# A macaron layer on one core: C spread by the matrix engine from three bf16 parts, expert results weighed where they leave PSUM, and gathered by an adding DMA

## The chip, the cores and the metric

The program runs on one core of one Trainium2 chip. The metric is the device time of one execution in microseconds (us). Its engines are TensorE (PE, with its weight loads as PEld), VectorE (DVE), ScalarE (ACT), GpSimd (POOL) and SyncE (SP), which only issues DMAs here. PE clock figures are shares of full speed as the profile shows them granted.

## What is computed

The input x holds 2 sequences of 2048 rows of 128 numbers. Three sublayers follow one another, each on the layer norm of x and added to it:

```
x = x + 0.5 * ffn(layernorm(x))     # 32 experts, 4 of them per row, and 4 shared chunks
x = x + ssm(layernorm(x))           # 256 channels, 16 states
x = x + 0.5 * ffn(layernorm(x))     # the same weights again

ffn: scores = softmax(x router^T); the best 4, divided by their sum
     out = sum over the 4 of weight * down(silu(gate x) * up x), plus the shared expert
ssm: u, z = silu(...); B, C = u W_x + b_x; dt = softplus(u W_dt + b_dt)
     h_t = h_{t-1} * exp(dt_t * A) + dt_t * u_t * B_t        # 16 states per channel
     y_t = sum over the 16 states of h_t * C_t, plus D * u_t; out = (y * z) W_out + b_out
```

All of it is in fp32.

## The kernel before

**Tiles.** x stays in SBUF as 8 blocks `xb[b]` of 512 rows (4 tiles of 128 rows). Blocks 0 to 3 are the first sequence, 4 to 7 the second.

**The expert sublayers** (`mixture`, L498) take the blocks in groups, `GROUPS` (L36): 0-1, 2-3 and 4-7 in the first, 0-3, 4-5 and 6-7 in the second. A group is routed on DVE (L548 to L720): every row's 4 experts, and for each a place in a list sorted by expert and padded so that 128 places have one expert. POOL scatters the normed rows `xn` to those places in `xs` in DRAM, one indirect DMA for each tile and choice (L761, 256 in all). The experts go in batches of 4 times 128 places (112 in all, 56 per sublayer): SP loads `xs` (L856), PE turns it (`pt_x`, L866), ACT copies it out of PSUM (L869), PE does gate and up in two halves (`gu`, L883), with the offsets of the weights loaded to registers from `sl` (L875), ACT does the silu (L895), DVE multiplies (L901), PE turns again (`pt_h`), ACT copies (L910), PE does down (`oq`, L915), ACT copies the result (L924), SP stores it to `ys`. Then POOL gathers the 4 results of each row (L944, 256 DMAs into `yg`), and DVE multiplies each with its weight `wk` and adds it to x (L958, 256 instructions). `wk` comes from L730 to L738. The shared expert (L797 to L836) adds to x on its own.

**The state space** (`state_space`, L1007) goes block by block. A prologue makes u, z, B and C (`ps_b`, L1049, 32 rows: 16 of B, 16 of C) and dt. B and C are stored to DRAM (L1068). For each of the 16 states, 128 steps over the 8 blocks: SP spreads the row of B over 128 partitions by a DMA from DRAM (`bs`, L1144) and the row of C too (`cs`, L1179); POOL multiplies dt*u by B (L1155, "drive"); ACT makes the two decays in PSUM (`da`, L1167); DVE runs two scans over 512 columns (L1194) and multiplies the states by C (L1207, 128x1024, `hst` and `cs` both in SBUF); PE adds the product, turned, to `y` in PSUM (L997). An epilogue gates, projects and adds to x.

**What sets the order.** Every piece is an `op` with an engine, a guessed cost, reads, writes and a priority. `Plan.run` (L147) plays them through once at build time and fixes each engine's order; the priorities in `FIRST`, `SECOND` and `BLOCKS` (L47 to L67) decide between pieces that could start at the same time. Each engine then runs its list strictly in order. `RINGS` (L38) gives the number of buffers of each kind; PSUM has 8 banks: `y` takes 2, `da` 2, `gu` 2, `w` (everything else) 2.

Of the kernel before, what the change touches and what calls it, by code (L numbers as in the profile page):

```python
# [29 lines left out]
S = 16  # L30
SQ = 4
# [7 lines left out]
    y=1, da=2, gu=2, w=2,  # L39
    xn=4, xnT=3, rt=1, lo=1, sc=1, mr=1, mk=1, cum=1, sm=1, route=3,  # L40
    shb=1, sg=2, hs=4, xs=3, xT=2, h=2, hT=2, yq=2, yg=2,
    pro=1, u=1, z=1, xnTs=1, t2=4, dt=2, dtu=2, bs=3, cs=3, hst=3,
# [5 lines left out]
    (-688.4, -610.7, (-1306.1, 24.95), 852.9, (-570.4, 166.01), (1470.8, 462.55)),  # L48
    (295.5, 12697.4, (-3985.4, 43.35), 4958.0, (-3337.9, 135.87), (-392.6, 253.65)),
    (15.1, -395.6, (12799.2, 79.27), -483.9, (-450.5, 7.10), (-438.3, 144.71)),  # L50
)
SECOND = (
    (-1574.4, -939.9, (652.6, 0.03), -1436.8, (-3869.3, 0.78), (2227.8, 203.49)),
    (-546.7, 12169.7, (3525.1, 83.68), -3253.9, (480.7, 378.95), (14344.2, 162.64)),
    (-1606.9, 12399.2, (902.0, 249.98), -512.2, (916.6, 0.00), (852.9, 148.58)),
# [3 lines left out]
    (-4279.5, 84.48),  # L59
    (-631.7, 0.50),  # L60
    (-608.5, 34.66),
    (64.0, 1.83),
    (-3035.2, 283.21),
    (-3171.2, 11.49),
    (-4049.9, 104.09),
    (-323.4, 156.10),
# [23 lines left out]
class Plan:  # L90
# [4 lines left out]
    NEAR, LAG, SWITCH, DMA, TURN, AGE = 0.0625, 0.2, 1.3, 2.3, 0.8000, 0.0900  # L95
# [106 lines left out]
def macaron_kernel(  # L202
# [41 lines left out]
        for k in ("y", "da", "gu", "w")  # L244
# [61 lines left out]
    xb = [load(f"x{b}", xf[b], [P, TB, D], (-1000, b)) for b in range(NBLK)]  # L306
# [28 lines left out]
    zero = buf("t2", [P, SQ * D], name="zero")  # L335
    op("dve", 0.5, lambda: nc.vector.memset(zero.t, 0.0), w=[zero], prio=(-1, 0))
    rows, buf_of = {}, {}
    for li, layer in enumerate(GROUPS):
        seen = {}
        for gi, blocks in enumerate(layer):  # L340
            n = len(blocks)
            k = seen.get(n, 0)
            seen[n] = k + 1
            buf_of[li, gi] = (n, k)
            if (n, k) not in rows:
                rows[n, k] = [dram_buf(f"{v}{n}{k}", [slots(blocks) * P, D]) for v in ("xs", "ys")]

    def clear_rows(key, prio):
        b = rows[key][0]
        v = b.t.rearrange("(c p r) d -> c p (r d)", p=P, r=SQ)  # L350
        for c in range(v.shape[0]):
            op(
                "sp",
                0.8,
                lambda c=c: nc.sync.dma_start(v[c], zero.t),
                r=[zero],
                p=[b],
                prio=prio,
                size=4 * P * SQ * D,
            )  # L360
# [10 lines left out]
    for i, key in enumerate(order_of_rows[1:]):  # L371
        clear_rows(key, (-900, 10 * i + 4))
# [4 lines left out]
    wx = load("wx", w_x, [P, ND, 2 * S], late)  # L377
    bx = load("bx", b_x, [2 * S, 1], late)
# [24 lines left out]
    nc.gpsimd.iota(iota_p.t, [[0, 1]], channel_multiplier=1, allow_small_or_imprecise_dtypes=True)  # L403

# [55 lines left out]
    def ln_apply(v, b, dst, prio, hold=()):  # L460
        mv, rs, nb, mvs, rss = stat[v]

        def f():
            for t in range(TB):
                i = b * TB + t
                nc.scalar.activation(
                    dst.t[:, t, :],
# [6 lines left out]
        op("act", 1.15, f, r=[xb[b], rss[b]], w=[dst], hold=hold, prio=prio)  # L474

    def transposed(src, ring, dst_ring, prio, name):
# [3 lines left out]
        def f():  # L480
            for t in range(TB):
                nc.tensor.transpose(pt.t[:, t, :], src.t[:, t, :], ident.t)
# [15 lines left out]
    def mixture(li, gi, pr):  # L498
# [7 lines left out]
        if li == 0:  # L506
            for b in blocks:
                op("dve", 1.75, lambda b=b: ln_stats(v, b), r=[xb[b]], w=[stat[v][3][b]], prio=p)
# [4 lines left out]
        for i, b in enumerate(blocks):  # L513
            xns[b] = buf("xn", [P, TB, D])
# [163 lines left out]
        idx_b, sl_b, wk_b = Buf(), Buf(), Buf()  # L678
# [4 lines left out]
        def indices():  # L683
# [5 lines left out]
            route["wk"] = sbuf[3].tile([P, NTM, TOPK], F32, tag="wk", name="wk")[:, :NT, :]  # L689
# [7 lines left out]
        def owners():  # L697
# [4 lines left out]
            nc.vector.tensor_scalar(ej, ej, float(E - 1), 3.0 * H, ALU.min, ALU.mult)  # L702

            den = sm_tile("den", [P, NTM])[:, :NT]
            nc.vector.tensor_reduce(den, sm["m8"][:, :NT, :TOPK], AX.X, ALU.add)
            nc.vector.reciprocal(den, den)
            nc.vector.tensor_scalar(den, den, 0.5, None, ALU.mult)

        op("dve", 1.3, owners, w=[smb], prio=p)
# [9 lines left out]
        def slot_list():  # L719
            nc.vector.tensor_copy(route["sl"], ejT.t[0:1, :NSL])  # L720

        op("dve", 0.25, slot_list, r=[ejT, route_b], w=[sl_b], prio=p)
        pw = pr["weigh"]

        for k in range(TOPK):
            eq = buf("lo", [P, NTM, E], name="eq", part=lambda t: t[:, :NT, :])

            def weigh(k=k, eq=eq):
                p8 = sm["p8"][:, :NT, :]
                nc.vector.tensor_tensor(  # L730
                    eq.t, posm.t, p8[:, :, k : k + 1].to_broadcast([P, NT, E]), ALU.is_equal
                )
                nc.vector.tensor_tensor(eq.t, eq.t, sc.t[:, :, :E], ALU.mult)
                nc.vector.tensor_reduce(route["wk"][:, :, k], eq.t, AX.X, ALU.add)
                if k == TOPK - 1:
                    wk = route["wk"]
                    den = sm["den"][:, :NT]
                    nc.vector.tensor_tensor(  # L738
                        wk, wk, den.unsqueeze(2).to_broadcast([P, NT, TOPK]), ALU.mult
                    )  # L740

            op(
                "dve",
                2.05 * f,
                weigh,
                r=[posm, sc, smb, route_b],
                w=[eq],
                p=[wk_b],
                hold=[turn_b],
                prio=pw,  # L750
            )
# [35 lines left out]
        for b in blocks:  # L787
# [3 lines left out]
            for c in range(NSH):  # L791
                w = w_all[:, E + c, :]
                gp, up = buf("gu", [P, T], name="gp"), buf("gu", [P, T], name="up")
# [27 lines left out]
            def down(o=o, hs=hs):  # L821
# [18 lines left out]
                w=[xb[b]],  # L840
# [6 lines left out]
        for q in range(NSL // SQ):  # L847
            pe_ = (*pr["experts"](q), q)
            xs = buf("xs", [P, SQ, D])
# [10 lines left out]
                size=4 * P * SQ * D,  # L860
# [3 lines left out]
            def turn(dst_, src_):  # L864
                for s in range(SQ):
                    nc.tensor.transpose(dst_.t[:, s, :], src_.t[:, s, :], ident.t)  # L866
# [3 lines left out]
            for s0 in range(0, SQ, 2):  # L870
                gu, sg = buf("gu", [P, 2, 2 * H], name="gu"), buf("sg", [P, 2, H], name="sgq")
# [52 lines left out]
            op("act", 0.59, lambda a=yq, b=o: nc.scalar.copy(a.t, b.t), r=[o], w=[yq], prio=pe_)  # L924
# [11 lines left out]
        for i, b in enumerate(blocks):  # L936
            for t in range(TB):
                pc = pr["combine"](i * TB + t)
                yg = buf("yg", [P, TOPK, D])
                for k in range(TOPK):  # L940

                    def gather(i=i, t=t, k=k, yg=yg):
                        pool(
                            nc.gpsimd.indirect_dma_start(  # L944
                                out=yg.t[:, k, :],
# [4 lines left out]
                                ),  # L950
                            )
                        )

                    op("pool", 1.26, gather, r=[ys_b, idx_b, route_b], p=[yg], prio=pc, lag=2.5)

                def add(i=i, b=b, t=t, yg=yg):
                    for k in range(TOPK):
                        nc.vector.scalar_tensor_tensor(  # L958
                            xb[b].t[:, t, :],
                            yg.t[:, k, :],  # L960
                            route["wk"][:, i * TB + t, k : k + 1],
                            xb[b].t[:, t, :],
                            ALU.mult,
                            ALU.add,
                        )
                    if li == 0:
                        ln_stats("b", b, t, t + 1)

                op(
                    "dve",  # L970
                    1.4 + (0.44 if li == 0 else 0.0),
                    add,
                    r=[yg, wk_b, route_b],
                    w=[xb[b]],
                    p=[stat["b"][3][b]] if li == 0 else [],
                    prio=pc,
                )
            if li == 1:
# [4 lines left out]
                    r=[xb[b]],  # L983
# [23 lines left out]
    def state_space(b, rank):  # L1007
# [36 lines left out]

        ps = buf("w", [2 * S, T], name="ps_b")

# [6 lines left out]
        bc = buf("t2", [2 * S, T], name="bc")  # L1053
# [12 lines left out]
        def store_b():  # L1066
            bd_t["t"] = rows2.tile([2 * S, T], F32, tag="bd", name="bd")
            nc.sync.dma_start(bd_t["t"], bc.t)  # L1068

        op("sp", 0.8, store_b, r=[bc], w=[bd], prio=pp, size=8 * S * T)  # L1070
# [66 lines left out]
        for s in range(S):  # L1137
# [24 lines left out]
            for k in range(ND):  # L1162
                da = buf("da", [P, T], place=ND * n + k)

                def decay(s=s, k=k, da=da):
# [9 lines left out]
            cb = buf("cs", [P, T], place=n)  # L1175
            op(
                "sp",
                0.8,
                lambda s=s, cb=cb: nc.sync.dma_start(  # L1179
                    cb.t,  # L1180
                    bd_t["t"][S + s : S + s + 1, :]
                    .rearrange("o t -> (o t)")
                    .partition_broadcast(P),
                ),
                r=[bd],
                w=[cb],
                prio=rank(s - 3),
                size=4 * P * T,
            )
            for k in range(ND):  # L1190
# [12 lines left out]
                op("dve", 1.3, scan, r=[das[k], st_b[s]], w=[h], prio=ps_)  # L1203
# [10 lines left out]
            op("dve", 1.6, times_c, r=[cb], w=[h], prio=ps_)  # L1214
# [24 lines left out]
        for i in range(2):  # L1239
# [57 lines left out]
            op("dve", 1.3, added, r=[po], w=[xb[b]], p=[stat["c"][3][b]], prio=pe_)  # L1297
# [69 lines left out]
```

## Time and profile before

| | before |
|---|---|
| median of 5 runs | 1641.74 us (1632.44 to 1642.64) |
| the profiled execution | 1642.64 us, span 1640.9 us, PE clock 0.80 |
| busy, us: PE / DVE / POOL / ACT | 1063.9 / 1031.5 / 905.7 / 812.4 |

The span is the time from the first to the last instruction; the 1.7 us around it belong to the launch. By the first and the last step of each block the span falls into four stages, and the profile gives the busy time of each engine in each of them:

| stage, us | what runs | PE | DVE | ACT | POOL |
|---|---|---|---|---|---|
| 0 to 393 | loads, routing, first group's experts | 245.5 | 134.4 | 125.7 | 158.0 |
| 393 to 814 | state space of blocks 0 to 3, experts of the first sublayer | 289.1 | 374.7 | 295.7 | 270.2 |
| 814 to 1348 | blocks 4 to 7, experts of the second sublayer | 358.4 | 435.1 | 306.0 | 345.8 |
| 1348 to 1641 | the last groups' experts | 170.9 | 87.4 | 85.0 | 131.8 |

### The profile page before, as it was taken

The page shows a single profiled execution, that of the slowest core. Times are in us where ns is not written, and L with a number is a line of the kernel's source. Part 1 is how long each engine was busy: PE and PEld are TensorE (multiplying, and loading weights), DVE is VectorE, ACT ScalarE, POOL GpSimd, SP SyncE. Part 2 cuts the span into 40 slices and gives each one's busy share as a digit, 9 for nine tenths or more (in the row PEclk, how much of TensorE's full clock was granted, in tenths as well). Part 3 has the DMA queues.
Part 4 walks back from the last instruction along what each step waited for, and adds up shares of the span by engine and source line. Part 5 has one row for each costly group of instructions (what it writes and reads, how often), then busy time and mean ns, then how long its engine had stood idle before and what let it go on. Part 6 is the DMA issues. An engine that isn't in the chain of part 4 may idle for free.

```text
span 1640.9 us, 18009 instructions
## 1 busy us (share of the span) xinstructions
PE 1063.9 (65%) x5202; PEld 792.4 (48%) x5202; DVE 1031.5 (63%) x1741; ACT 812.4 (50%) x1428; POOL 905.7 (55%) x702
## 2 busy tenths in 40 slices
PE   6496184777666778682767753575778786186781
PEld 3264072555555556571444432454567565165561
DVE  5346032243989989988798779748989955022232
ACT  3242061247877759781572652256778844043320
POOL 1605607266557755738664778655894463714435
PEclk9698597898989879795777975587979987687896
DMA  9812132244455436543331133224555532234422
GB/s 306 314 52 71 53 98 67 75 106 138 142 143 150 139 90 168 146 125 97 89 98 54 57 102 106 86 66 133 152 155 161 155 92 72 71 100 111 120 65 51
DMA packets 204257, 187.81 MB, mean 114 GB/s; under 512 B 18690, under 2 KB 155523, under 8 KB 204163
## 3 DMA queue, kind: packets, MB, share of 16 engines
q1 hardware_dynamic: 187778, 153.09, 31.8%
q0 software_dynamic: 16384, 33.59, 7.2%
q8 instruction: 45, 0.74, 0.2%
q14 instruction: 50, 0.40, 0.1%
HBM read 123.16 MB, written 63.44 MB: 114 GB/s over the span
## 4 chain that ended last, share of the span: by engine, by line
PE 31%; DVE 27%; issue 17%; another core or an unknown queue 11%; ACT 8%; POOL 2%; DMA 2%; SPq 1%; DVEq 0%; POOLq 0%; ACTq 0%
DVE hst L1194 11%; PE gu L883 8%; DVE hst L1207 4%; PE oq L915 4%; PE o L824 3%; DVE x L958 3%; PE gp L797 2%; PE up L797 2%; ACT L294 2%; PE pt_h L866 2%; PE pt_x L866 2%; PE ps_o L1281 2%; PE y L997 2%; DVE h L901 1%
## 5 line engine op out<-in xcount | busy, mean ns | idle before, releaser
L1155 POOL TENSOR_TENSOR hst<-dtu,bs 128x1024 f32<-128x1024 f32 x128 | 307.4, 2411 | 218.2 <-PE y L997 171.6
L761 POOL DMA_INDIRECT xs<-xn,idx x256 | 272.0, 1062 | 238.9 <-DVE le L699 78.1
L944 POOL DMA_INDIRECT yg<-ys,idx x256 | 254.3, 993 | 243.4 <-DVE x L958 147.8
L883 PE MATMUL gu<-w_all,xT 128*128 x896 | 271.0, 438 | 44.3 <-DVE h L901 27.6
L997 PE MATMUL y<-ident,hst 128*128 128x128 f32 x1024 | 168.0, 319 | 179.2 <-DVE hst L1207 161.4
L1207 DVE TENSOR_TENSOR hst<-hst,cs 128x1024 f32<-128x1024 f32 x128 | 276.1, 2157 | 3.6
L901 DVE TENSOR_TENSOR h<-sgq,gu 128x256 f32<-128x256 f32 x224 | 89.1, 414 | 294.9 <-ACT sgq L895 193.5
L1194 DVE TENSOR_TENSOR_SCAN hst<-da,st,hst 128x512 f32<-128x512 f32 x192 | 237.6, 1267 | 13.5 <-ACT da L1167 12.9
L997 PEld LDWEIGHTS y<-ident,hst 128*128 128x128 f32 x1024 | 140.1, 166 | 217.7 <-issue 217.3
L1167 ACT ACTIVATE da<-dt,a 128x512 f32<-128x512 f32 x256 | 172.8, 688 | 110.5 <-DVE hst L1194 106.0
L883 PEld LDWEIGHTS gu<-w_all,xT 128*128 128x128 f32 x896 | 182.9, 222 | 84.2 <-DVE h L901 32.8
L915 PE MATMUL oq<-w_all,hT 128*128 x896 | 142.0, 309 | 103.2 <-ACT hT L910 55.4
L915 PEld LDWEIGHTS oq<-w_all,hT 128*128 128x128 f32 x896 | 128.4, 217 | 131.3 <-ACT hT L910 72.6
L294 ACT ACT_TABLE_LOAD x144 | 184.8, 1283 | 3.3 <-PEq L1355 0.8
L895 ACT ACTIVATE sgq<-gu 128x256 f32<-128x256 f32 x224 | 82.3, 384 | 136.5 <-PE gu L883 61.5
L958 DVE SCALAR_TENSOR_TENSOR x<-yg,wk,x 128x128 f32<-128x128 f32 x256 | 121.9, 477 | 33.0 <-DMA yg<-ys,idx 26.8
L924 ACT COPY yq<-oq 128x512 f32<-128x512 f32 x112 | 65.2, 583 | 121.3 <-remote 68.3
L866 PE MATMUL pt_h<-ident,h 128*128 128x128 f32 x448 | 84.7, 311 | 51.8 <-DVE h L901 23.7
L806 ACT ACTIVATE sg<-gp 128x512 f32<-128x512 f32 x64 | 38.2, 597 | 152.1 <-PE gp L797 87.3
L910 ACT COPY hT<-pt_h 128x512 f32<-128x512 f32 x112 | 65.1, 584 | 83.9 <-PE pt_h L866 43.9
L866 PEld LDWEIGHTS pt_h<-ident,h 128*128 128x128 f32 x448 | 61.2, 160 | 78.2 <-issue 35.0
L812 DVE TENSOR_TENSOR hs<-sg,up 128x512 f32<-128x512 f32 x64 | 44.1, 690 | 84.1 <-PE up L797 37.8
(133 smaller groups left out, 1438.7 us busy)
## 6 DMA issues: line engine op xcount, KB each, us to landing
bs<-bd SPq DMA_DIRECT2D x128, 256.0 KB
cs<-bd SPq DMA_DIRECT2D x128, 256.0 KB
xs<-xs SPq DMA_DIRECT2D x112, 256.0 KB
ys<-yq SPq DMA_DIRECT2D x112, 256.0 KB
xs<-zero SPq DMA_DIRECT2D x56, 256.0 KB
xs<-xn,idx POOLq DMA_INDIRECT x256
yg<-ys,idx POOLq DMA_INDIRECT x256
x<-in_x SPq DMA_DIRECT2D x8, 256.0 KB
```

The lines of the kernel that those rows point to most:

```text
L294: nc.scalar.preload_act_table_set(name)
L761: nc.gpsimd.indirect_dma_start(out=xs_b.t, out_offset=bass.IndirectOffsetOnAxis(ap=route["idx"][:, i * TB + t, k : k + 1], axis=0), in_=xn ...
L866: nc.tensor.transpose(dst_.t[:, s, :], src_.t[:, s, :], ident.t)
L883: nc.tensor.matmul(gu.t[:, s, :], xT.t[:, s0 + s, :], w_flat[:, bass.ds(offs["v"][s0 + s], 2 * H)], start=True, stop=True,)
L915: nc.tensor.matmul(o.t[:, s, :], hT.t[:, s, :], w_flat[:, bass.ds(offs["v"][s] + 2 * H, D)], start=True, stop=True,)
L944: nc.gpsimd.indirect_dma_start(out=yg.t[:, k, :], out_offset=None, in_=ys_b.t, in_offset=bass.IndirectOffsetOnAxis(ap=route["idx"][:, i * ...
L958: nc.vector.scalar_tensor_tensor(xb[b].t[:, t, :], yg.t[:, k, :], route["wk"][:, i * TB + t, k : k + 1], xb[b].t[:, t, :], ALU.mult, ALU.add,)
L997: nc.tensor.matmul(y[:, t, k * P : (k + 1) * P], src[:, k, t * P : (t + 1) * P], ident.t, is_transpose=True, start=start and k == 0 and t ...
L1155: nc.gpsimd.tensor_tensor(h.t[:, :, 1:], dtu.t, bs.t.unsqueeze(1).to_broadcast([P, ND, T]), ALU.mult)
L1167: nc.scalar.activation(da.t, dt.t[:, k, :], AF.Exp, scale=a_t.t[:, k, s : s + 1])
L1194: nc.vector.tensor_tensor_scan(h.t[:, k, 1:], da.t, h.t[:, k, 1:], 0.0 if ini else st_sb[:, k, s : s + 1], ALU.mult, ALU.add,)
L1207: nc.vector.tensor_tensor(h.t[:, :, :T], h.t[:, :, 1:], cb.t.unsqueeze(1).to_broadcast([P, ND, T]), ALU.mult,)
```

## The change

1. **C by PE.** `W_x` and its bias are laid out so that the product has 128 rows: C, B, C and C, each at the start of a quarter. The three copies of C become three bf16 parts that add up to C (two more ACT copies and two DVE subtractions per block). For each step one bf16 matmul with a matrix of zeros and ones adds the three parts and spreads them over 128 partitions of PSUM (`c`, one bank). L1179 goes; the multiplication reads C from PSUM.
2. **Weights travel with the rows.** Rows of `xn` and `xs` have 160 numbers, 128 and the 32 weights of the experts (zero where not chosen). L730 to L738 go; a shorter calculation writes the weights before the scatter. After the down matmul, ACT loads four column numbers to registers and evicts each 128x128 tile with the weight as its scale.
3. **Adding gather.** The gather adds to x in SBUF. `yg` and L958 go. The four adds to a tile of x are ordered, since each writes it; the order of issue is choice by choice over the four tiles of a block.
4. **PSUM and rings.** `gu` joins `w`: together 3 banks instead of 2 and 2; `c` takes the eighth. `hst` and `xs` have 4 buffers instead of 3. The tables of priorities and four constants of the plan have other numbers, and the zeros for `xs` are stored after the late weights.

The core of the diff:

```diff
-    y=1, da=2, gu=2, w=2,
+    y=1, da=2, c=1, w=3,
...
-    shb=1, sg=2, hs=4, xs=3, xT=2, h=2, hT=2, yq=2, yg=2,
-    pro=1, u=1, z=1, xnTs=1, t2=4, dt=2, dtu=2, bs=3, cs=3, hst=3,
+    shb=1, sg=2, hs=4, xs=4, xT=2, h=2, hT=2, yq=2,
+    pro=1, u=1, z=1, xnTs=1, t2=4, dt=2, dtu=2, bs=3, cm=2, hst=4,
...
+            nc.vector.scalar_tensor_tensor(
+                wt.t, posm.t, 0.0, sc.t[:, :, :E], ALU.is_gt, ALU.mult
+            )
...
+                nc.vector.tensor_tensor(
+                    xns[b].t[:, :, D:], wt.t[:, t, :],
+                    sm["den"][:, t].unsqueeze(2).to_broadcast([P, TB, E]), ALU.mult,
+                )
...
-            op("act", 0.59, lambda a=yq, b=o: nc.scalar.copy(a.t, b.t), r=[o], w=[yq], prio=pe_)
+            def weighed(q=q, yq=yq, o=o, xs=xs):
+                _, cols = nc.values_load_multi_w_load_instructions(
+                    route["sw"][0:1, q * SQ : (q + 1) * SQ],
+                    engines=[ET.Activation],
...
+                for s in range(SQ):
+                    nc.scalar.activation(
+                        yq.t[:, s, :], o.t[:, s, :], AF.Copy,
+                        scale=xs.t[:, s, bass.ds(cols[s], 1)],
+                    )
...
+            for k in range(TOPK):
+                for t in range(TB):
+                            nc.gpsimd.indirect_dma_start(
+                                out=xb[b].t[:, t, :], 
...
+                                compute_op=ALU.add,
...
+        op("act", 0.65, lambda: nc.scalar.copy(cm.t, bc.t), r=[bc], w=[cm])
+            nc.vector.tensor_tensor(bc.t[v], bc.t[v], cm.t[v], ALU.subtract)
+            lambda: nc.scalar.copy(cm.t[P // 2 :], bc.t[P // 2 :]),
+            nc.vector.tensor_tensor(cm.t[v], bc.t[v], cm.t[v], ALU.subtract)
...
-            cb = buf("cs", [P, T], place=n)
+            cb = buf("c", [P, T], place=n)
+                "pe", 0.33,
+                lambda s=s, cb=cb: nc.tensor.matmul(
+                    cb.t, pick.t[:, s : s + 1].to_broadcast([P, P]), cm.t, start=True, stop=True,
+                ),
+                r=[cm, dt], w=[cb], prio=rank(s - 1),
```

## The prediction

> **What bounds the kernel now.** I read, in this order: the busy times by stage, the groups of instructions, the single lines, the timeline of a stretch where the state space runs almost alone, and the chain that ended last. In the middle stages (393 to 814 and 814 to 1348 us) DVE is the busiest engine, 374.7 of 421 us (89%) and 435.1 of 534 (81%). The two groups it can shed are these (busy us, mean ns, then idle time before):
>
> ```profile
> L1207 DVE TENSOR_TENSOR hst<-hst,cs 128x1024 f32<-128x1024 f32 x128 | 276.1, 2157 | 3.6
> L958 DVE SCALAR_TENSOR_TENSOR x<-yg,wk,x 128x128 f32<-128x128 f32 x256 | 121.9, 477 | 33.0 <-DMA yg<-ys,idx 26.8
> ```
>
> The lines of L1207 and L812 (min/median/max) and the timeline say why the first is dear:
>
> ```profile
> L1207 DVE TENSOR_TENSOR hst<-hst,cs x128: 1195/1908/6247, 401.4 to 1318.5; 128x1024 f32<-128x1024 f32 x128
> ```
> ```profile
> L812 DVE TENSOR_TENSOR hs<-sg,up x64: 657/687/894, 20.8 to 1603.4; 128x512 f32<-128x512 f32 x64
> ```
> ```profile
> 981.50 2.35 POOL L1155 TENSOR_TENSOR hst<-dtu,bs 128x1024 f32<-128x1024 f32 x1 [1.36 <-PE y L997]
> 981.67 3.27 DVE L1207 TENSOR_TENSOR hst<-hst,cs 128x1024 f32<-128x1024 f32 x1
> ...
> 984.86 2.44 DVE L1194 TENSOR_TENSOR_SCAN hst<-da,st,hst 128x512 f32<-128x512 f32 x2
> ...
> 987.17 2.33 POOL L1155 TENSOR_TENSOR hst<-dtu,bs 128x1024 f32<-128x1024 f32 x1 [1.36 <-PE y L997]
> 987.34 3.25 DVE L1207 TENSOR_TENSOR hst<-hst,cs 128x1024 f32<-128x1024 f32 x1
> ```
>
> The reader is to see that the multiplication, 1.20 us at best, takes 3.27 when POOL's drive started 0.17 us earlier: 2.18 us of drive left, then 1.09 of its own. The drive itself hardly stretches (2.35). So two SBUF operands on DVE wait for a POOL operation. L812, with one operand in PSUM, spreads only from 0.66 to 0.89.
>
> ACT is next, 295.7 and 306.0 us in these stages, 144 table loads of 1.28 us over the span among them. PE has 289.1 and 358.4, at a clock of 0.83 and 0.78. In the first and last stage nobody is full; there the chain waits mostly for PE's hand-offs while POOL sends one scatter or gather after another (its largest share there, 27% and 23%, is "another core or an unknown queue"). The scatters and gathers stay as many, so I leave these stages as they are.
>
> **The change, part by part.** The sums are made against the profiled execution, 1642.6 us (span 1640.9 and 1.7 around it), 0.9 above the median of 1641.7.
>
> *C from PSUM.* L812 takes 0.69 us for 512 columns and L901 0.41 for 256, so 1.08 ns a column and 1.24 us for 1024; L1207's own minimum is 1.20. I take 1.23. DVE loses 123.0 - 64 x 1.23 = 44.3 us in the second stage and 153.1 - 78.7 = 74.4 in the third. Nothing else of a step becomes shorter: the scans (1.27 us) read their decay from PSUM already. The spread on PE, one bf16 matmul of 512 columns, lies between 0.34 us (mean of L600 and L623, mostly 256 columns, bf16) and 0.69 (L797, 512 columns, fp32). I take 0.45, so 29 us of PE in each stage. Its output has one bank, so the matmul of a step waits on PE until the multiplication before it has ended, and everything listed behind it on PE (the 8 turns of `y`, expert matmuls) waits too. Its cover is the next two scans, 2.46 us; `y` costs 1.06 to 1.94 us of that, so the cover holds unless an expert's matmuls come between. 128 DMAs of C leave the SP queue and 33 MB leave the DMA engines; their share was 0.47 and 0.37, so no gain. The bf16 parts cost 16 subtractions of about 0.69 us (as L812) on DVE, 5.5 us a stage, and 16 copies of 0.585 us (as L924) on ACT, 4.7 a stage. They run beside the making of dt, which has three dependent POOL operations of 1.5 us per half.
>
> *The adding gather.* L958 goes: 49.6 us of DVE in the second stage, 22.0 in the third. The DMA's issue on POOL stays at about 0.95 us and one each 1.25. Now a gather landed 1631.93 to 1634.50, 2.57 us after its issue began. An addition has no row here. From below it is 2.57 us; from above I take twice that. One tile gets its next addition four issues later, 5.0 us, so up to there POOL doesn't wait; I take 3 us and a cost of nothing. The cover is the four tiles taken in turn; without it each wait would hold the drives behind it in POOL's list.
>
> *The weights.* L730, L733, L734 and L738 are 38 us in all, some 13 of them in the third stage; what replaces them is six operations like L670 (0.74) and sixteen like L528 (0.29), 9 us. It now stands ahead of the scatter, about 2 us per group, on the path for the first and last group: +4 us.
>
> *Eviction with a scale.* One copy of 0.585 us becomes four tiles of 128 columns and one register load. The nearest row is L466, 128 columns with two pointer operands: 8 in 3.18 us, 0.40 each. From below, L895 and L924 extrapolate to 0.28. The register load has a row on PE:
>
> ```profile
> L875 PEldq TENSOR_LOAD <-sl x112: 327/332/814, 122.2 to 1568.5; - x112
> ```
>
> So the batch costs ACT between 4 x 0.28 - 0.585 = +0.55 us (load hidden) and 4 x 0.40 + 0.33 - 0.585 = +1.34. I take +1.1, so 34 batches give 37 us in the second stage, 28 give 31 in the third.
>
> The Trainium skill has a rule on each side here. "ScalarE: Activation LUTs", What ACT_TABLE_LOAD costs, gives 186 ns plus 0.833 per column, 93 more for a pointer operand and an overlap of 93, an estimate of 1.27 us for the four. "DMA: Bandwidth & Descriptors", Latency and other measured facts, puts the floor of a `tensor_load` at some 600 ns, which speaks against the change; L875's median of 332 is below that. By the two pages together the batch would be +1.28 us and the sum 11 us later.
>
> *PSUM and rings, zeros.* `xs` rows grow by a quarter: 56 clears of 256 KB become 320, 3.7 MB more, 12 us at the 306 GB/s of the first slice, but most now come after the weights; I take 0, bounds 0 and 12. `hst` with 4 buffers lets the drive run further ahead: POOL waited 171.6 us for PE's `y`. PSUM with 3 shared banks instead of 2 and 2 costs from nothing (a batch in the last stage takes 97 us / 16 = 6.1) to rival 2; I take 0.
>
> *Sum.* Second stage: DVE 374.7 - 44.3 - 49.6 + 5.5 = 286; ACT 295.7 + 37 + 4.7 = 337; PE 318. ACT becomes the busiest. At the fill that the busiest engine has now (0.89), 337 us take 379: **-42 us**. Third stage: DVE 435.1 - 74.4 - 22.0 - 9 + 5.5 = 335, ACT 342, POOL 346, PE 387 at the present clock. At the present fill of 0.815 the stage lasts 420 us if ACT decides and 475 if PE does; I take the middle, 448: **-86**. Other stages: +4 for the weights, -3 for L958 behind the last gather. 1642.6 - 42 - 86 + 1 = 1515.
>
> **Rivals.**
>
> 1. *More: DVE stays the bound and the rest gets out of its way.* Then all that DVE sheds in the middle is gained: 118.7 + 71.6 + 9 - 11 = 188 us, 1455; with the waits of POOL for L958 in the last stage (105 us, of which a quarter may be on the path) about 1430. For it: where the state space runs alone (965 to 1049 us) a step takes 5.66 us and would take 2.46 + 1.23 = 3.7. Against it: ACT at 78% between 400 and 500 us already.
> 2. *Slower: three PSUM banks.* All evictions share three banks, and each now waits behind longer lists on ACT and DVE. A batch holds banks (matmuls, eviction, hand-offs, estimated from L866, L883, L915, L901 and the new eviction) for about 10.6 us, so 3.5 us a batch with three banks, under the 6.1 it takes in the last stage. It begins to decide when waits for ACT and DVE raise that beyond 18. The gain of 127 us is eaten from 1.15 us more per batch (112 batches); at 1.6 us more the time is 1694.
> 3. *Nothing: slow additions.* If an addition lands after 7 us instead of 5, POOL waits 2 us in each of 64 rounds of four, 128 us with the drives behind them: 1643. Against it: packets of 512 bytes keep the DMA engines at a third of their time.
> 4. *It doesn't free the multiplication.* If a PSUM operand waits for POOL as well, the first part gives nothing and the sum is about 1580. L812's narrow spread speaks against it.
>
> **How the numbers follow.** The forecast and rival 4 (1455 to 1600) have 0.58, rival 1 (below 1455) 0.20, rival 3 and mixtures (1600 to 1650) 0.10, rival 2 (above) 0.12. A measurement can tell about 0.5%, 8 us, from no change. Faster: 0.58 + 0.20 + 0.05 = 0.83; same 0.04; slower 0.13. The range of 8 in 10 goes from 1400 (some 0.07 below) to 1640 (some 0.14 above).
>
> **What would show it.** Right: the multiplication at 1.2 to 1.3 us with hardly any spread; steps of about 3.7 us where the state space is alone; no L958; ACT the busiest engine between 400 and 700 us, a batch's four evictions 1.2 to 1.6 us; POOL not waiting for its own DMAs. Wrong: PE waiting for the multiplication with expert work behind it, ring waits on `w`, additions that land later than 5 us, or a first stage that lasts longer than 393 us.

## The result, and the profile after

The kernel after takes 1650.6 us (median of 52 runs, 1640.4 to 1659.0) against 1643.9 for before (94 runs, 1628.3 to 1658.2). The ratio is 1.0048, interval 1.0037 to 1.0060: a hair slower, where 1515 was predicted. The profiled execution has a span of 1645.7 us.

The page of after, the busy times, the queue of POOL's DMAs and six groups (busy us, mean ns, then idle time before them):

```profile
PE 1047.8 (64%) x5324; PEld 781.4 (47%) x5330; DVE 786.4 (48%) x1453; ACT 908.1 (55%) x1804; POOL 1013.4 (62%) x706
...
q0 software_dynamic: 49152, 37.78, 12.4%
...
L1010 POOL DMA_INDIRECT x<-ys,idx x256 | 397.6, 1553 | 185.5 <-DMA ys<-yq 79.9
L1252 POOL TENSOR_TENSOR hst<-dtu,bs 128x1024 f32<-128x1024 f32 x128 | 306.8, 2408 | 156.0 <-PE y L1060 118.7
L810 POOL DMA_INDIRECT xs<-xn,idx x256 | 248.9, 972 | 237.1 <-DVE xn L793 75.5
...
L984 ACT ACTIVATE yq<-oq,xs 128x128 f32<-128x128 f32 x448 | 128.1, 372 | 124.3 <-PE oq L964 46.2
...
L1304 DVE TENSOR_TENSOR hst<-hst,c 128x1024 f32<-128x1024 f32 x128 | 156.2, 1220 | 29.6 <-issue 18.2
...
L1276 PE MATMUL c<-cm,pick 128*128 128x512 bf16 x122 | 50.7, 415 | 134.3 <-DVE hst L1304 115.8
```

DVE lost 245 us of its 1031.5, and the multiplication is what it was meant to be. The line of L1304 alone (min/median/max) shows that no spread is left, where L1207 had 1195/1908/6247. The line of the gathers has a new figure on POOL instead (first before's gather and queue, then after's gather):

```profile
L1304 DVE TENSOR_TENSOR hst<-hst,c x128: 1191/1223/1225, 434.3 to 1312.1; 128x1024 f32<-128x1024 f32 x128
```
```profile
L944 POOL DMA_INDIRECT yg<-ys,idx x256: 938/944/1962, 312.6 to 1631.9; - x128
q0 software_dynamic: 16384, 33.59, 7.2%
...
L1010 POOL DMA_INDIRECT x<-ys,idx x256: 1532/1542/2054, 341.6 to 1637.9; - x128
```

So at the median an adding gather holds POOL 0.60 us longer, 154 us in all, and the queue of POOL's DMAs moves 49152 packets where before had 16384. POOL is now busier than DVE.

The busy times of after by stage, first drive and ends of blocks 3 and 7 as bounds, as in the prediction (columns: us, then PE, PEld, DVE, ACT, POOL busy, clock, DMA share, GB/s):

```profile
0.00:424.60 424.60, 244.78 (x1089) 169.87 (x1090) 111.69 (x420) 144.09 (x312) 183.48 (x185) 0.77 0.45 132
424.60:798.90 374.30, 273.38 (x1576) 214.70 (x1576) 282.20 (x336) 316.22 (x599) 237.90 (x124) 0.91 0.40 101
798.90:1336.30 537.40, 375.93 (x1849) 272.48 (x1853) 348.78 (x559) 347.89 (x637) 373.79 (x246) 0.81 0.33 85
1336.30:1645.70 309.40, 153.70 (x815) 124.35 (x813) 43.77 (x140) 99.94 (x257) 218.26 (x154) 0.74 0.46 95
```

Against before the first stage lasts 31 us longer (425 for 393), the second 46 less (374 for 420), the third 2.7 more (537.4 for 534.7), the last 17 more (309 for 292). The second stage did what was predicted in its length (46 us less, 42 predicted). The third gave nothing although DVE sheds 87 us in it, and POOL has 374 us of work there. The last is nearly all gathers: 128 of them, 1.84 us apart, are 236 of its 309 us.

### The profile page after: what moved, and what is told of

Its sections match the earlier page's. It is cut to its first block, busy times and chain, and to the rows that moved or that the text cites. A ratio compares the mean times of both kernels' runs of the same rounds, so it can differ in the third digit from the quotient of the medians.

```text
span 1645.7 us, 18352 instructions
## 1 busy us (share of the span) xinstructions
PE 1047.8 (64%) x5324; PEld 781.4 (47%) x5330; DVE 786.4 (48%) x1453; ACT 908.1 (55%) x1804; POOL 1013.4 (62%) x706
## 3 DMA queue, kind: packets, MB, share of 16 engines
q0 software_dynamic: 49152, 37.78, 12.4%
## 5 line engine op out<-in xcount | busy, mean ns | idle before, releaser
L1010 POOL DMA_INDIRECT x<-ys,idx x256 | 397.6, 1553 | 185.5 <-DMA ys<-yq 79.9
L810 POOL DMA_INDIRECT xs<-xn,idx x256 | 248.9, 972 | 237.1 <-DVE xn L793 75.5
L932 PE MATMUL gu<-w_all,xT 128*128 x896 | 255.2, 421 | 75.4 <-ACT yq L984 25.8
L984 ACT ACTIVATE yq<-oq,xs 128x128 f32<-128x128 f32 x448 | 128.1, 372 | 124.3 <-PE oq L964 46.2
L1304 DVE TENSOR_TENSOR hst<-hst,c 128x1024 f32<-128x1024 f32 x128 | 156.2, 1220 | 29.6 <-issue 18.2
L1060 PE MATMUL y<-ident,hst 128*128 128x128 f32 x1024 | 153.1, 299 | 8.3 <-DVE hst L1304 8.3
L1276 PE MATMUL c<-cm,pick 128*128 128x512 bf16 x122 | 50.7, 415 | 134.3 <-DVE hst L1304 115.8
L915 PE MATMUL pt_x<-ident,xs 128*128 128x128 f32 x448 | 73.5, 294 | 67.1 <-DMA xs<-xs 43.4
L918 ACT COPY xT<-pt_x 128x512 f32<-128x512 f32 x112 | 64.8, 595 | 69.1 <-PE pt_x L915 45.3
L915 PEld LDWEIGHTS pt_x<-ident,xs 128*128 128x128 f32 x448 | 55.6, 151 | 83.3 <-issue 42.7
```

The source lines that it names most:

```text
L810: nc.gpsimd.indirect_dma_start(out=xs_b.t, out_offset=bass.IndirectOffsetOnAxis(ap=route["idx"][:, i * TB + t, k : k + 1], axis=0), in_=xn ...
L915: nc.tensor.transpose(dst_.t[:, s, :], src_.t[:, s, :P], ident.t)
L932: nc.tensor.matmul(gu.t[:, s, :], xT.t[:, s0 + s, :], w_flat[:, bass.ds(offs["v"][s0 + s], 2 * H)], start=True, stop=True,)
L984: nc.scalar.activation(yq.t[:, s, :], o.t[:, s, :], AF.Copy, scale=xs.t[:, s, bass.ds(cols[s], 1)],)
L1010: nc.gpsimd.indirect_dma_start(out=xb[b].t[:, t, :], out_offset=None, in_=ys_b.t, in_offset=bass.IndirectOffsetOnAxis(ap=route["idx"][:, i ...
L1060: nc.tensor.matmul(y[:, t, k * P : (k + 1) * P], src[:, k, t * P : (t + 1) * P], ident.t, is_transpose=True, start=start and k == 0 and t ...
```

## The experiments

Three things were to be told apart at first: **theory 1**, that POOL's time for the adding gathers ate the gain; **theory 2**, that the experts' evictions and the shared PSUM banks did; and **theory 3**, that the new order of the pieces is a bad one whatever a gather costs. In the second set theory 2 stands for any other chain that holds the time. One such chain took shape when the trace was read for PE: while POOL sends plain scatters or gathers 1.26 us apart, PE's results reach the other engines late. The timeline of after beside scatters (start, duration, idle time before):

```profile
1437.26 2.07 PE L932 MATMUL gu<-w_all,xT 128*128 x4 [12.81 <-issue]
1437.41 0.96 POOL L810 DMA_INDIRECT xs<-xn,idx  x1 [0.30 <-issue]
...
1445.93 0.38 ACT L944 ACTIVATE sgq<-gu 128x256 f32<-128x256 f32 x1 [8.72 <-remote]
...
1455.05 0.59 ACT L959 COPY hT<-pt_h 128x512 f32<-128x512 f32 x1 [8.74 <-remote]
...
1455.68 2.07 PE L964 MATMUL oq<-w_all,hT 128*128 x8 [16.35 <-issue]
```

PE ends `gu` at 1439.3 and ACT starts on it at 1445.9; the turned `h` reaches ACT at 1455. I call a *stall* each stretch between PE's last matmul and a semaphore update of PE that comes more than 1.5 us behind it, and add the stretches up: 171 us in before (104 beside scatters, 42 beside gathers, 26 beside both), 141 in after (115 beside scatters, 16 beside both, 5 beside adding gathers).

**Four parts changed one at a time**, each kernel in its own order.

```diff
# after_no_add
-                                compute_op=ALU.add,
# after_copy_evict: in place of four weighed evictions
+            nc.scalar.copy(yq.t, o.t)
# after_c_sbuf: the second operand of times_c
-                    cb.t.unsqueeze(1).to_broadcast([P, ND, T]),
+                    dt.t,
# before_add: the gather adds into one of two zeroed buffers
+                                compute_op=ALU.add,
```

> The changed kernel in its own order, the gather writing to x in place of adding (the additions are left out, so x holds the last of the four rows). Theory 1, the adding DMA is dear on POOL (1.54 us of issue against 0.94 before, one each 1.85 us against 1.25): POOL sheds 256 x 0.6 = 154 us, of it about 19 us ahead of the first block, 38 us ahead of block 4 and 77 us at the end lie on the path, so about 1515 us. Theory 2, the experts' evictions and the three shared PSUM banks eat the gain: within 15 us of the changed kernel, 1635 to 1650. Theory 3, the new order of the pieces is a bad one whatever a gather costs: less than 50 us faster.

> The changed kernel in its own order, with the eviction of a batch as one plain copy of 512 columns and no register load (the weights are left out). ACT sheds about 0.9 us per batch, 100 us in all. Theory 1 (POOL): at most 20 us faster, since POOL is full at the end. Theory 2 (evictions and banks): 60 us faster or more. Theory 3: less than 20 us.

> The changed kernel in its own order, with the multiplication by C reading dt from SBUF in place of C from PSUM (the product with C is left out; the spread is still made). If the PSUM operand is what frees the multiplication from POOL, L1304 goes from 1.22 us back to 1.9 to 2.4 us and the kernel is 50 to 120 us slower. If the first part gives nothing on the path, it is within 15 us.

> The kernel before in its own order, with its gathers adding into two lasting buffers in place of writing into yg (what the weights multiply is then a running sum, so the result is another). Theory 1: the gather's issue goes from 0.94 to 1.54 us on POOL, and the kernel is 60 to 130 us slower. Theories 2 and 3: within 15 us of the kernel before.

Measured: after_no_add 1735.2 us, 1.056 of before (1.050 to 1.062); after_copy_evict 1630.4, 0.989 (0.984 to 0.993); after_c_sbuf 1726.4, 1.048 (1.041 to 1.055); before_add 1647.5, 1.002 (0.999 to 1.005). The groups that answer, of after_no_add, after_c_sbuf and before_add:

```profile
L1010 POOL DMA_INDIRECT x<-ys,idx x256 | 245.2, 958 | 251.2 <-DMA ys<-yq 123.0
```
```profile
L1304 DVE TENSOR_TENSOR hst<-hst,dt 128x1024 f32<-128x1024 f32 x128 | 252.8, 1975 | 3.5
```
```profile
L949 POOL DMA_INDIRECT held<-ys,idx x256 | 406.6, 1588 | 135.0 <-DVE x L964 46.9
```

The operand in PSUM is worth 76 us (1726 against 1650) in one and the same order: the first part works. The Trainium skill, "GPSIMD Engine Reference", 1. Specifications, has POOL contend with DVE instructions that read two SBUF inputs; 1.22 us against 1.98 agrees. The weighing on ACT costs 20 us, far from the 60 that theory 2 asked for. But after_no_add and before_add contradicted theory 1 as I had it. In after_no_add POOL got 152 us back, and the time rose by 85 instead of falling. PE's stalls rose from 141 to 269 us, 137 of them beside gathers alone; in before_add they fell from 171 to 105 while POOL paid 152 us more, and the time stayed the same, as if the two had cancelled. So an adding gather seems to have a price and a benefit.

**Price and stalls apart**, all four on after, in its own order.

```diff
# after_dearer_gather, behind every gather; after_spaced_scatter, behind every scatter
+                        for _ in range(2):
+                            pool(nc.gpsimd.tensor_tensor(scr.t, scr.t, scr.t, ALU.add))
# after_no_add_spaced: the same behind every gather, and
-                                compute_op=ALU.add,
# after_add_scatter, in the scatter
+                                compute_op=ALU.add,
```

> The kernel after in its own order, with two small in-place additions on POOL (128x144, by the row of 1.27 us for 128x512 about 0.35 us each) after each of the 256 adding gathers, so that a gather takes about 2.5 us of POOL in place of 1.85; the result is unchanged. If POOL's time for the gathers is what the end of stages 3 and 4 hangs on (theory 1: POOL's price), 180 us more of it must show nearly whole where gathers fill POOL: 90 us in the last stage alone less the 80 us that POOL idles there, and some 40 in stage 3, together 1700 us or more. If POOL's price is covered and the time is held by other chains (theory 2), 1650 to 1670 us.

> The kernel after in its own order, with plain gathers (the addition to x is left out) and the same two small POOL operations after each, so that gathers are again about 1.9 us apart, but move rows as packets of 4096 B. If PE's late hand-offs beside plain gathers (137 us of stalls in after_no_add) come of how densely POOL issues them, the stalls beside gathers fall under 40 us and the time comes to 1650 us, give or take 25. If they come of the plain gather's large packets, the stalls stay above 100 us and the time is 1735 us or more.

> The kernel after in its own order, with the two small POOL operations after each of the 256 scatters (about 1.9 us apart in place of 1.26; 180 us more work on POOL; the result is unchanged). If dense issue makes PE's hand-offs late, the 115 us of stalls beside scatters fall under 40 us, and the time is 1600 to 1660 us in spite of POOL's added work. If density is not the cause, the stalls stay near 115 us and the time goes to 1690 us or more.

> The kernel after in its own order, with the scatters made adding DMAs too (into rows that were cleared once; the second sublayer's rows then hold the first's as well, which nothing clears). If an adding DMA costs POOL 1.55 us and moves packets of 512 B whatever its direction, a scatter goes from 0.97 to about 1.55 us. If PE's late hand-offs go with dense issue or large packets, the 115 us of stalls beside scatters fall under 40 us, and the time is 1600 to 1660 us; if neither, POOL's 150 us more are paid in stages 1 and 4 and the time is 1690 us or more.

| | us | ratio to before | stalls, us |
|---|---|---|---|
| after_dearer_gather | 1856.2 | 1.128 (1.122 to 1.134) | 121 |
| after_no_add_spaced | 1706.3 | 1.037 (1.031 to 1.043) | 178 (3 to 20 beside gathers) |
| after_spaced_scatter | 1685.5 | 1.025 (1.019 to 1.031) | 0 |
| after_add_scatter | 1610.1 | 0.979 (0.973 to 0.984) | 0 |

The added operations of after_dearer_gather were dearer than expected:

```profile
L1021 POOL DMA_INDIRECT x<-ys,idx x256 | 399.8, 1562 | 138.6 <-DMA ys<-yq 61.9
...
L1032 POOL TENSOR_TENSOR scr<-scr 128x144 f32<-128x144 f32 x512 | 374.8, 732 | 20.1
```

395 us of POOL (with the idle time before them) made the kernel 206 us longer, 0.52 us for each. By that slope the 154 us that the addition costs POOL are 80 us of time, an estimate. This speaks for theory 1 after all, with a price that after_no_add had hidden under new stalls: in after_no_add_spaced, with gathers 2.07 us apart, at most 20 us of stalls are left beside them. Its time missed the 1650 us expected, though: it is 56 us above after. Gathers 0.22 us further apart than after's (56 us of POOL, 29 us by the slope) and 37 us more of stalls, beside scatters above all, would come to about that (an estimate). Stalls beside scatters go the same way, to nothing at 2.1 us between scatters and at 1.85 us with the addition. In after_add_scatter the DMA engines are busier than in after (0.72 against 0.25 of the time between 150 and 230 us), so it is not their load that holds PE up. after_spaced_scatter lost its stalls but took 1685 us where 1600 to 1660 was expected: POOL paid 220 us for it.

**A shorter pause, an order with the true price, and C alone.**

```diff
# before_tiny: behind every scatter and gather; after_tiny_scatter: behind every scatter; scr is 128x16
+                        pool(nc.gpsimd.tensor_tensor(scr.t, scr.t, scr.t, ALU.add))
# after_price_told, in the planner's costs, with other tables
-                        1.26,
+                        1.85,
# before_c_only, on before with other tables: C's parts, banks and this operand
-            cb = buf("cs", [P, T], place=n)
+            cb = buf("c", [P, T], place=n)
```

> The kernel before in its own order, with one tiny in-place addition on POOL (128x16) after each of its 256 scatters and 256 gathers; the result is unchanged. The addition is estimated at 0.15 to 0.25 us, from 0.43 us for 128x144, so that POOL gets some 100 us of work more. If PE's late hand-offs come of indirect DMAs issued back to back, one short instruction of another kind between them ends the stalls (171 us in before, under 30 here) and the time is 1540 to 1600 us. If they come of the spacing of 1.26 us as such, spacing of 1.45 us changes them little (over 100 us left), and the time is 1640 to 1690 us.

> The kernel after in its own order, with the same tiny addition on POOL after each of the 256 scatters alone; the result is unchanged. By the first theory (back to back) the 141 us of PE's late hand-offs fall under 20 us and the time is 1590 to 1625 us, the 1610 of the adding scatters being had at some 100 us less POOL work. By the second (spacing as such) over 80 us of stalls stay and the time is 1640 to 1680 us.

> The kernel after, whose planner is told what was measured: 1.85 us of POOL for an adding gather in place of 1.26 (landing 1.8 us later in place of 2.8), 1.65 us for a weighed eviction in place of 1.25, 1.6 us for the normalisation of a block in place of 1.15; and tables of priorities found anew for these prices. The work is that of after. If the third stage lost its gain because the order was drawn up with a gather too cheap by a third (the 48 gathers ahead of block 4's dt), the time is 1560 to 1610 us. If POOL's price itself is what is paid, whatever the order, 1630 to 1660 us.

> The kernel before with the first part of the change alone: C spread by PE from three bf16 parts and read from PSUM by the multiplication, with banks as in after; rows, gathers (plain) and the weighing on DVE as in before, and tables of priorities found anew, since the given ones leave the planner without a next step. If the multiplication of 1.23 us is worth what I predicted of stages 2 and 3 (42 and 86 us) and only the adding gather took it back, the time is 1500 to 1560 us. If the steps are held by something else (late hand-offs beside plain gathers and scatters), 1590 to 1640 us.

Measured: before_tiny 1566.1 us, 0.960 of before (0.954 to 0.965), stalls 67; after_tiny_scatter 1576.1, 0.965 (0.960 to 0.970), stalls 51; after_price_told 1584.6, 0.969 (0.964 to 0.974), stalls 128; before_c_only 1599.0, 0.977 (0.971 to 0.982), stalls 153. Beside scatters after_tiny_scatter runs like this:

```profile
1382.49 0.98 POOL L821 DMA_INDIRECT xs<-xn,idx  x1 [0.17 <-issue]
1382.77 0.42 PEld L927 LDWEIGHTS pt_h<-ident,h 128*128 128x128 f32 x4 [1.51 <-DVE h L962]
1382.77 0.66 PE L927 MATMUL pt_h<-ident,h 128*128 128x128 f32 x4 [0.79 <-DVE h L962]
1383.50 0.22 POOL L833 TENSOR_TENSOR scr<-scr 128x16 f32<-128x16 f32 x1
...
1385.41 2.01 PE L944 MATMUL gu<-w_all,xT 128*128 x4 [1.98 <-issue]
```

A pause of 0.22 us behind each DMA, 1.40 us from one to the next, takes most of the stalls away, not all as I expected. It makes both kernels some 4% faster, so they still stand level: the stalls cost both and don't explain the lost gain. With the gather's price told, the planner finds an order that is 3.6% faster (1.0048 to 0.969) for the same work. The time lies in the range that was expected, but not for the reason given: block 4's first drive comes 165 us after block 3's last multiplication (96 in after), with 33 gathers and 64 scatters ahead of it, and each of the four stages is only 11 to 20 us shorter. So it shows that the order matters, not that the untold price spoilt it. before_c_only came out in the range for steps that are held by something else.

**The parts with fewer late hand-offs**, all with the pause of before_tiny and tables of the same search.

```diff
# after_plain_tiny: plain gathers into a buffer of their own (xs and bs a buffer shorter), and on DVE
+                        nc.vector.tensor_tensor(
+                            xb[b].t[:, t, :], yg.t[:, k, :], xb[b].t[:, t, :], ALU.add
+                        )
# after_price_told_tiny: the pause behind scatters alone
```

> The kernel before, without any part of the change, with the tiny additions after every scatter and gather, and tables of priorities found by the search that served the other replanned kernels (told 2.1 us for the multiplication and 1.6 us for the normalisation). It is the control: if the order given to before was as good as the search finds, 1550 to 1580 us (before_tiny took 1566); if a new order is by itself worth what the changes seemed to give, 1530 us or less.

> The kernel before with the spreading of C alone (before_c_only) and the tiny additions after every scatter and gather. If the multiplication from PSUM gives what was predicted once neither late hand-offs nor an adding gather are in its way, 1500 to 1530 us (66 us under before_c_only's 1599 for the hand-offs alone would be 1533). If the steps hang on something else, 1550 us or more.

> The kernel after with its gathers plain: they land in a buffer of their own, and DVE adds them to x unweighed (four additions for each tile of tokens); C's spreading and the weighing at eviction stay; the tiny additions are after every scatter and gather; two rings are one buffer shorter to make room, and the tables are found anew. If the adding DMA is a loss because POOL is nearer to the bound than DVE (0.6 us of POOL at 0.5 us per us, against DVE's added work), 1480 to 1520 us and below after_price_told_tiny. If DVE's additions cost as much as they did in before, 1530 to 1560 us.

> The kernel after with its planner told the measured prices (after_price_told, 1585 us) and the tiny additions after every scatter: the whole change, in a right order, without late hand-offs. If order and hand-offs are separate losses, 1585 less 74, 1505 to 1530 us. If the hand-offs were part of what the right order had already gone around, 1550 us or more.

Measured: before_replanned_tiny 1612.9 us, 0.983 of before (0.980 to 0.987); before_c_only_tiny 1527.9, 0.932 (0.928 to 0.936); after_plain_tiny 1627.0 (1604.2 to 1631.8), 0.992 (0.990 to 0.995); after_price_told_tiny 1565.3, 0.953 (0.949 to 0.958). The first is the control: the same work as before_tiny in an order of my search takes 47 us more (39 by the two ratios). That is outside both ranges expected. So 47 us is what another order can do by itself, and smaller differences between replanned kernels say nothing. C alone is 85 us under the control and 38 under before_tiny. The 38 are no more than an order can do; the 85, and after_c_sbuf in one order, show what C is worth. With the pause it **beats both kernels**: 1528 us. The other two parts, in either form, gave nothing on top of it in the orders tried. after_plain_tiny is outside both ranges expected. For after_price_told_tiny the second one came true: the pause gained only 19 us on after_price_told, and its stalls fell only from 128 us to about 90.

Where C alone gains, by stage (first drive, ends of the last multiplications of blocks 3 and 7):

| | first | second | third | last |
|---|---|---|---|---|
| before | 393.5 | 400.8 | 525.4 | 321.2 |
| after | 424.6 | 363.4 | 525.3 | 332.4 |
| before_tiny | 340.5 | 407.0 | 529.0 | 285.3 |
| after_tiny_scatter | 373.1 | 364.9 | 518.2 | 318.5 |
| before_replanned_tiny | 360.0 | 422.1 | 533.3 | 288.9 |
| before_c_only_tiny | 369.2 | 342.2 | 458.7 | 355.6 |
| after_price_told_tiny | 390.9 | 346.3 | 519.8 | 307.6 |

The second and third stage of before_c_only_tiny are 135 us shorter than before_tiny's and 154 shorter than the control's; the first and last are 99 and 76 longer. Part of the work that ran beside the longer steps is done outside them now: in the last stage PE has

```profile
1170.10:1525.70 355.60, 253.35 (x1316) 197.26 (x1316) 111.93 (x326) 126.28 (x254) 195.16 (x324) 0.83 0.36 99
```

1316 matmul instructions, against 975 in the last stage of before_tiny and 863 in the control's.

## Why the prediction was wrong, point by point

By stage, the 132 us between the predicted 1515 and the profiled execution lie mostly in the third: it changed by +3 us where -86 stood in the sum, which is 89 us. The first and last stage together missed by 47 us (+31 and +17, where +4 and -3 stood). The second came 4 us better than predicted.

**C from PSUM: right.** 1.22 us was measured for 1.23 predicted, PE's matmul took 0.42 us for 0.45, steps in the stretch 978 to 1037 us take 3.70 us at the median (3.89 on average) for about 3.7, and rival 4 fell. In that stretch of after's timeline the multiplication starts 0.45 us behind a drive and ends within it:

```profile
999.75 2.35 POOL L1252 TENSOR_TENSOR hst<-dtu,bs 128x1024 f32<-128x1024 f32 x1
...
1000.20 1.22 DVE L1304 TENSOR_TENSOR hst<-hst,c 128x1024 f32<-128x1024 f32 x1
```

The wait of PE for the multiplication is there (115.8 us), but it is covered: the multiplication itself waits for PE's matmul 1.2 us in all.

**The adding gather: a step that failed.** "The DMA's issue on POOL stays at about 0.95 us and one each 1.25. ... I take 3 us and a cost of nothing." The issue takes 1.54 us and comes each 1.85. I had bounded when an addition lands, and had asked whether POOL would wait for it; it doesn't (0.3 us of idle time before an issue). What grew is the issue itself. I had held that price fixed, without a bound, where before had no row for an adding DMA. 154 us of POOL at 0.52 are some 80 of the 132 us (an estimate: the slope comes from work added to POOL, and the run without the addition gave no time back, since it stalled more). No run shows this share directly.

**The third stage: -86 became +3, the larger step that failed.** The sum took the stage as filled by its busiest engine, at the fill of before, and divided. But block 4 doesn't start when block 3 ends: it starts when the last expert batch of its group is stored and its rows are gathered. That batch is stored at 739 us in before, 55 us ahead of block 3's last multiplication, and at 780 in after, 8 us ahead of it. Then POOL's list puts 50 gathers (39 and 11) ahead of the two halves of block 4's `dt`, from 782 to 880 us (the expectation of after_price_told counted 48). POOL alone in the timeline of after, 770 to 888 us:

```profile
782.15 1.57 POOL L1010 DMA_INDIRECT x<-ys,idx  x1 [7.30 <-DMA ys<-yq]
...
853.63 1.86 POOL L1218 TENSOR_TENSOR w<-w,ea 128x512 f32<-128x512 f32 x1
...
878.42 2.02 POOL L1010 DMA_INDIRECT x<-ys,idx  x1 [0.30 <-issue]
879.87 1.86 POOL L1218 TENSOR_TENSOR w<-w,ea 128x512 f32<-128x512 f32 x1
...
884.49 4.66 POOL L1252 TENSOR_TENSOR hst<-dtu,bs 128x1024 f32<-128x1024 f32 x2
```

The first drive is at 884, 96 us after the last multiplication of block 3; in before it is at 807, 13 us after. So this wait grew by 83 us. The 64 steps behind it did get quicker: from the first drive to the last multiplication they take 429 us, for 512 in before. What they gained, 83 us, the wait took. Of the 83, 47 us are the later batch, and 50 gathers dearer by 0.6 us are 30 more (an estimate). Why the batch comes later was not found: the 28 batches up to it take 316 us for 286, but 313 with plain evictions (after_copy_evict) and 367 beside slow steps (after_c_sbuf), so neither the weighing nor quicker steps explain it. A wait of 65 us or more stands there in every kernel with C from PSUM (711 to 804 us in before_c_only_tiny, with plain gathers), so the adding gather's price alone didn't make it. It doesn't forbid a gain either: before_c_only_tiny has the wait and yet the shortest third stage; its 64 steps take 366 us, in which PE runs 1206 matmul instructions, for 1569 in after.

**The order, put at nothing.** The tables of priorities changed with the kernel, and the sum has no term for them. The same work as in after, in the order of after_price_told, takes 66 us less. How much of the miss is the order given to after can't be told apart from its price and its waits.

**First and last stage: "as many, so I leave these stages as they are".** Scatters and gathers stay as many, but the gathers are dearer: 32 before the first drive and 128 in the last stage, so 19 and 77 us of POOL. The first drive came 31 us later, the last stage took 17 us more. That the gathers did it is argued: before_c_only_tiny, with plain gathers in another order, has its first drive 29 us later than before_tiny too.

**Eviction: +1.1 us per batch was right** (four in 1.14 us and about 0.5 before them, for 0.59), and off the path for the most part: 20 us when taken back. (By its own figures the prediction's estimate of 1.27 us for the four is 1.26.)

**Rivals.** Rival 1 didn't come: DVE was relieved and the time stayed. PSUM's three banks (rival 2) were not tested alone; `gu` waits 25.8 us in all for the eviction that frees a bank, and before_c_only_tiny has the same banks and is the fastest kernel here. Rival 3 had the right place, POOL and its gathers, with the wrong mechanism: not late landing, a dear issue. Its 1643 came close by another sum, which is luck.

**Open.** Why PE's hand-offs come late beside dense indirect DMAs: spacing ends it and the load of the DMA engines doesn't cause it; the path between was not found. The profile models the ends of matmuls, so whether the matmul itself or its update is late isn't shown either. And what the weighing at eviction and the adding gather are each worth in a good order: both together came out 37 us above C alone, the weighing with plain gathers 99 us (with two rings a buffer shorter), against 47 that an order can do.

## What to carry to other kernels

When a DMA is given more to do, price its issue on the engine that issues it before its landing; for an adding gather of 128 rows that was 1.54 us against 0.94. Where stages are joined by a chain of other work, experts and gathers here, time taken out of one stage is gained only if what the next one waits for comes earlier too. Read the hand-offs of PE beside bursts of indirect DMAs: here one tiny instruction between them was worth 4%, in the kernel before as in the one after.

## What the runs showed that was not expected

- An adding indirect DMA costs POOL 1.54 us for 128 rows, gathering or scattering; a plain one costs 0.94 to 0.97. With the addition left out the queue's 49152 packets became 20480, so the addition makes 112 more of each gather.
- PE's semaphore updates come up to 37 us late while plain indirect DMAs follow each other 1.26 us apart. Stalls beside scatters in after: 115 us at 1.26, 48 at 1.40 with a tiny instruction between, none at 2.1, and none with adding scatters at 1.85.
- A small POOL addition (128x144, two behind each DMA) takes 0.73 us on average behind an adding gather and 0.44 behind a plain one.
